# Layer 1's normalised batches: 32x32 block turns on VectorE and copies within SBUF in place of TensorE transposes

## The chip, the core and the metric

The kernel runs on one core of a Trainium2 chip. A core has five engines with instruction streams of their own: TensorE (PE, matrix products, with a separate record PEld for its weight loads), VectorE (DVE), ScalarE (ACT), GpSimd (POOL) and SyncE (SP, which here issues nearly all DMAs). They meet only through semaphores. Data lies in SBUF (128 partitions), matrix products land in PSUM (banks of 128 x 512 f32), and DMAs move data between device memory and SBUF or within SBUF. The metric is the time of one execution on the device in microseconds, median of the runs.

## What is computed

Two transformer layers with adaptive layer norm, on x of 4 batches x 512 tokens x 512 features, all in f32. The change touches layer 1 only:

```python
h = _layernorm(x) * (1 + ca) + sa            # "h" of the attention
x = x + ga * _L1_attn_ref(h, w_q, w_k, w_v, w_o)   # 32 heads of 128, 8 key/value heads, causal, softmax
h = _layernorm(x) * (1 + cb) + sb            # "h" of the FFN
x = x + gb * _L1_ffn_ref(h, gate, up, down)  # silu(h gate^T) * (h up^T), then down^T; width 1792, int weights
```

`sa, ca, ga, sb, cb, gb` are rows of 512 per batch, from a small product with the condition vector. The norm runs over the features of a token. A token sits in a partition when x is normalised, but the matrix products want the features in the partitions, so each normalised batch (512 x 512) has to be turned: 16 blocks of 128 x 128.

## The kernel before

Layer 0 comes first (to about 184 us of the span) and is not touched. Layer 1's attention follows (184 to about 1720 us), then the FFN (to the end). Inside each the order of every engine's instructions is written out by hand (`tc.manual_schedule`): an instruction stands in its engine's queue where the Python code emits it.

**Attention.** The 32 pairs of batch and key/value head are blocks n = 0 to 31 (`NBLK`), b = n // 8, g = n % 8. A block has four query heads; two windows per block handle two heads each: window 2n ("even") and window 2n+1 ("odd"). `window` walks through 9 slots. In slot i it emits the score product of one token tile (`score`: PE product, DVE mask and maximum, ACT exponential), the division of the tile before (`divide`), the 32x32 block turn of the tile two before (`flip`, DVE); in slots 8 and 9 the two products with the values of the previous pair (`value`, tile `av`). Into the slots it spreads a list `fill` of further PE pieces, as evenly as its length allows, and a list `side` of work for other engines. Pieces of the even window are the query projection of block n+1 and a part of a key or value projection; pieces of the odd window are the seven products of the output projection of block n-1 (`o_pieces`; each product is one of the seven of a Strassen scheme, tile `quarter`) and up to three key or value pieces (`now`). A PE piece writes one of three PSUM banks (`bank`, pool `ps_sc`), which DVE or ACT then reads. After a window's slots, `carry` issues 16 DMAs on SP (L918) which move the turned probabilities of a pair within SBUF, 32 partitions x 4 runs of 1 KB each.

Every batch after the first has its layer norm made while the batch before is still in the attention. At g = 4 the batch is read back from device memory (`get`, L990, into tile `xn`). At g = 5 its moments are taken in the even window and ACT normalises it in place (`norm_pieces`, L1004); in the odd window `turn_pieces` puts four pieces among the PE fill, each of four TensorE transposes (L1035, tile `lnT`, one PSUM bank) and an ACT instruction (L1038) that scales, shifts and writes a quarter of `hT`. The fill of every odd window has four places for such pieces; in the blocks without them the places hold empty functions. The tiles `hT` come from a pool of four.

**FFN.** `ffn_exact` goes through the batches; for each, 14 hidden blocks n of 128 (`hidden`). An iteration emits the `gate` and `up` products of block n (8 + 8 products of 512 columns: four chunks of features, each in a high and a low part; L1349), then the `down` products of block n-1 (8, L1368). The chain of block n on the other engines is: ACT sigmoid (L1355), DVE two products (L1356, L1357), ACT rounding to the high part (L122), DVE the low part (L123). PSUM holds four accumulators of 512, one bank for turns (`ps_tr2`) and three banks for gate and up (`ps_hu`). The matrix products of batch b+1 need its normalised, turned, split batch `h2`; `prepare(b + 1)` returns a list of pieces, of which iterations n = 2 on emit one each, behind the products: n = 2 to 5 moments of a token tile, n = 6 the reciprocal deviation (one power on POOL, L68, between two small DVE instructions), n = 7 and 8 the normalisation on ACT (L1306, two tiles each, into the free space of `acc`), n = 9 to 12 one chunk each: four TensorE transposes (L1314), DVE scale and shift (L1318), ACT high part, DVE low part. For batch 0 the same iterations also carry the last batch's attention output (`leave_attention`, POOL additions L972 to L978 and L969, DVE L965) and weight loads with their conversion on POOL (L1338).

Of the kernel before, what the change touches and what calls it, by code (L numbers as in the profile page):

```python
# [8 lines left out]
F32 = mybir.dt.float32  # L9
# [8 lines left out]
P = 128  # L18
# [15 lines left out]
def adaln_two_layers(ctx: ExitStack, tc: tile.TileContext, a, out: bass.AP):  # L34
# [69 lines left out]
    def modulated_T(xn, b, m, shift, scale, hT, on_act, trp):  # L104

        def put(c, pt, sc_, sh_):
            if on_act[c] == "a":
                nc.scalar.activation(hT[:, c, :], pt, AF.Identity, bias=sh_, scale=sc_)
            else:
                nc.vector.tensor_scalar(hT[:, c, :], pt, sc_, sh_, ALU.mult, ALU.add)  # L110

        transposed(xn, b, m, shift, scale, put, trp)
        return hT

    def layernorm_T(b, m, shift, scale, pool, xnp, trp):
        xn = normalized(b, lambda: xnp.tile([P, NT, E], F32, tag="xn", name="xn"))
        hT = pool.tile([P, KC, S], F32, tag="hT", name="hT")
        return modulated_T(xn, b, m, shift, scale, hT, "vava", trp)

    def halves(hi, lo, t):  # L120

# [613 lines left out]
    def bank(shape, name):  # L735
        return ps_sc.tile(shape, F32, tag="sc", name=name)
# [255 lines left out]
    def one_x():  # L992
        return lnp.tile([P, NT, E], F32, tag="xn", name="xn")

    def norm_pieces(xb):
# [7 lines left out]
        def xn(t):  # L1003
            nc.scalar.activation(  # L1004
                xb[:, t, :], xb[:, t, :], AF.Identity,
                bias=out_["nmr"][:, t : t + 1], scale=out_["rstd"][:, t : t + 1],
            )
# [16 lines left out]
        return out_, side + after  # L1024

    def turn_pieces(b, got):

        m = modT[1]

        def piece(c):  # L1030
            if c == 0:
                h1[b] = hp.tile([P, KC, S], F32, tag="hT", name="hT")
            pt = bank([P, S], "lnT")
            for t in range(NT):
                nc.tensor.transpose(  # L1035
                    pt[:, t * P : (t + 1) * P], got["xn"][:, t, c * P : (c + 1) * P], ident
                )
            nc.scalar.activation(  # L1038
                h1[b][:, c, :], pt, AF.Identity,
                bias=m[:, 0, c, b : b + 1], scale=m[:, 1, c, b : b + 1],  # L1040
            )
            if c == KC - 1:
                sums_h(b, (nc.gpsimd, nc.gpsimd))

        return [lambda c=c: piece(c) for c in range(KC)]

    def small_loads():
        nc.sync.dma_start(gus[:, 0], a["L1_ffn_gate_scaleT"])
# [126 lines left out]
    load("v", 1)  # L1175
    pending = []
    begun = []

    for n in range(NBLK):
        b, g = divmod(n, HKV)  # L1180
# [12 lines left out]
        if g == 1 and b > 0:  # L1193
            sums, ends = leave_attention(b - 1, nc.gpsimd, gap, "ga", xb)
            side[0] = sums + 3 * [lambda: None] + ends
            side[1] = put(b - 1, xb)
        if g == HKV - 4:
            xb = one_x()
            side[1] = get(after, xb)
        if g == HKV - 3 and after or n == NBLK - 2:  # L1200
            got, side[0] = norm_pieces(xb)
            if after:
                turns_ = turn_pieces(after, got)
        if 0 < n <= len(pieces):
            found = scan(n - 1)
            side[1] += [lambda j=j: look(n - 1, j, found[j]) for j in range(2)]
# [7 lines left out]
        if n == 0:  # L1214
            window(0, q[:6])
        elif ahead:
            late = [lambda: load("q", n + 2)] if n + 2 < NBLK else []
            if n == 1:
                window(2, q, side[0], late)
            else:  # L1220
                window(2 * n, begun[:2] + q[:2] + begun[2:] + q[2:], side[0], late)
                begun = []
                if 2 * (m + 1) < NBLK:
# [24 lines left out]
        if 0 < n < NBLK - 2:  # L1248
            sums_in("q", n + 2)
        if n == 0:  # L1250
            sums_in("v", 1)
            begun = v_pieces(1)
            window(1, q[6:] + k_pieces(1) + begun[:3], (), [lambda: load("q", 2)])
            begun = begun[3:]
            sums_in("q", 2)
            load("k", 2)
            pending.append(("k", 2))
        else:
            if n > 1 and n + 2 < NBLK:
# [21 lines left out]
    def ffn_exact():  # L1281
        with (
# [11 lines left out]
            def prepare(b):  # L1294


                (st, mv), d, m = moments(), {}, modT[1]
                xn = osum.rearrange("p a b c -> p (a b c)")[:, : NT * E]
                xn = xn.rearrange("p (t e) -> p t e", e=E)

                def dev():
                    d["dev"] = deviation(mv)

                def norm(t):
                    rstd, nmr = d["dev"]
                    nc.scalar.activation(  # L1306
                        xn[:, t, :], x[b][:, t, :], AF.Identity,
                        bias=nmr[:, t : t + 1], scale=rstd[:, t : t + 1],
                    )

                def chunk(c):
                    pt, t = ps_tr2.tile([P, S], F32, tag="tr", name="lnT"), temp()
                    for i in range(NT):
                        nc.tensor.transpose(  # L1314
                            pt[:, i * P : (i + 1) * P], xn[:, i, c * P : (c + 1) * P], ident
                        )
                    sc_, sh_ = m[:, 3, c, b : b + 1], m[:, 2, c, b : b + 1]
                    nc.vector.tensor_scalar(t, pt, sc_, sh_, ALU.mult, ALU.add)  # L1318
# [180 lines left out]
```

## Time and profile before

| | us |
|---|---|
| median of 3 runs (lowest, highest) | 2040.57 (2040.56, 2052.83) |
| the profiled execution: its time / its span | 2043.52 / 2041.6 |
| PE busy / DVE / ACT / POOL | 2006.0 / 1363.2 / 878.8 / 759.5 |
| attention, 184 to 1680: length / PE busy | 1496.00 / 1493.06 |
| FFN, batch 1 (1800.88 to 1878.90): length / PE busy | 78.02 / 78.02 |
| mean granted TensorE clock, of full speed | 0.991 |

The span runs from the first to the last instruction of the profiled execution. A line of the page's list of groups gives the source line, the engine, the operation, output and input tiles with shapes, the count, the busy time and the mean duration, and then how long the engine was idle just before these instructions and who ended that. Timelines give start and duration in us. A merged timeline row "x4" is four instructions; the start of the next row says when the engine went on.

### The profile page before, as it was taken

How to read it: one execution, taken by the hardware profiler on the slowest of the kernel's cores; microseconds unless marked ns; L12 is line 12 of the kernel's file. 1: busy time of each engine (PE TensorE's matmuls, PEld its weight loads, DVE VectorE, ACT ScalarE, POOL GpSimd, SP SyncE). 2: the span in 40 equal slices, each digit the busy share in tenths (PEclk: the TensorE clock that was granted, in tenths of full speed). 3: DMA queues.
4: the chain of work that ended last, by engine and by line, in shares of the span. 5: the costliest groups of instructions: out<-in, count | busy, mean ns of one | idle time of the engine just before them, and what ended most of it. 6: DMA issues, size and time to landing. Idle time of an engine off the chain costs nothing.

```text
span 2041.6 us, 27493 instructions
## 1 busy us (share of the span) xinstructions
PE 2006.0 (98%) x9219; PEld 1571.0 (77%) x9219; DVE 1363.2 (67%) x3317; ACT 878.8 (43%) x2001; POOL 759.5 (37%) x659
## 2 busy tenths in 40 slices
PE   6999999999999999999999999999999999999998
PEld 4555777878788777778787778788777777888887
DVE  6957776676667766766676676667666674755554
ACT  4521554444444444544444444444444454323322
POOL 2316243334346343354463334346343333800000
PEclk8999999999999999999999999999999999999999
DMA  9322566666666756566766665667656656500000
GB/s 316 105 68 99 134 173 162 145 165 148 168 159 179 185 148 165 145 167 159 180 181 155 145 165 141 155 149 175 169 136 155 145 127 213 187 21 6 16 22 22
DMA packets 243640, 288.59 MB, mean 141 GB/s; under 512 B 23250, under 2 KB 184018, under 8 KB 243492
## 3 DMA queue, kind: packets, MB, share of 16 engines
q1 hardware_dynamic: 242964, 285.71, 53.5%
q8 instruction: 76, 1.25, 0.3%
q10 hardware_dynamic: 528, 1.05, 0.1%
q14 instruction: 72, 0.59, 0.1%
HBM read 142.99 MB, written 11.57 MB: 76 GB/s over the span
## 4 chain that ended last, share of the span: by engine, by line
PE 89%; DVE 1%; ACT 1%; SPq 0%; DMA 0%; issue 0%; ACTq 0%
PE quarter L746 47%; PE av L928 14%; PE sc L878 13%; PE p_gate L1349 5%; PE p_up L1349 5%; PE acc L1368 5%; PE lnT L1035 0%; PE lnT L1314 0%; SPq L918 0%; DMA x<-p 0%; DVE nmx L881 0%; ACT x L883 0%; DVE x L1377 0%; ACT tm L1089 0%; DVE tm L1376 0%
## 5 line engine op out<-in xcount | busy, mean ns | idle before, releaser
L878 PE MATMUL sc<-kT,qT 128*128 128x512 f32 (+3 forms) x1024 | 355.4, 433 | 0.8 <-DVE qT L778 0.8
L928 PE MATMUL av<-x,v 128*128 128x512 f32 x1008 | 293.7, 435 | 2.0 <-DMA x<-p 2.0
L928 PEld LDWEIGHTS av<-x,v 128*128 128x128 f32 x1008 | 189.4, 191 | 107.6 <-issue 63.3
L881 DVE TENSOR_REDUCE nmx<-sc 128x1 f32<-128x512 f32 (+3 forms) x512 | 251.3, 491 | 17.7
L893 ACT ACTIVATE x<-x,rden 128x512 f32<-128x512 f32 (+3 forms) x256 | 143.7, 561 | 237.5 <-DVE rden L892 237.5
L778 DVE TENSOR_TENSOR qT<-qT,quarter 128x512 f32<-128x512 f32 x224 | 150.4, 683 | 137.9 <-PE quarter L746 133.1
L893 ACT ACTIVATE p<-p,rden 128x512 f32<-128x512 f32 (+3 forms) x256 | 143.7, 562 | 223.3 <-DVE rden L892 221.8
L879 DVE TENSOR_TENSOR sc<-sc,mask 128x128 f32<-128x128 f32 x512 | 144.9, 283 | 135.0 <-PE sc L878 134.2
L842 DVE TENSOR_TENSOR acc<-acc,quarter 128x512 f32<-128x512 f32 x196 | 134.4, 686 | 132.5 <-PE quarter L746 132.4
L230 POOL TENSOR_TENSOR sq<-wq 128x512 f32<-128x512 f32 x32 | 41.1, 1284 | 477.1 <-DMA wq<-in_L_attn_w_q_dram 458.6
L878 PEld LDWEIGHTS sc<-kT,qT 128*128 128x128 f32 x1024 | 182.7, 191 | 25.5 <-DVE qT L778 1.2
L746 PEld LDWEIGHTS quarter<-wo,oT 128*128 128x128 f32 x744 | 140.9, 190 | 43.9 <-issue 20.1
L883 ACT ACTIVATE p<-sc,nmx 128x512 f32<-128x512 f32 (+3 forms) x256 | 134.9, 527 | 87.0 <-DVE nmx L881 78.6
L746 PE MATMUL quarter<-wo,oT 128*128 128x256 f32 x744 | 171.1, 379 | 0.2 <-ACT oT L933 0.2
L883 ACT ACTIVATE x<-sc,nmx 128x512 f32<-128x512 f32 (+3 forms) x256 | 134.8, 526 | 69.9 <-DVE nmx L881 65.3
L933 ACT COPY oT<-av 128x512 f32<-128x512 f32 x128 | 74.2, 579 | 163.9 <-PE av L928 162.0
L896 DVE STREAM_TRANSPOSE p<-p 128x512 f32<-128x512 f32 (+3 forms) x256 | 129.3, 505 | 1.8
L896 DVE STREAM_TRANSPOSE x<-x 128x512 f32<-128x512 f32 x248 | 124.8, 503 | 1.4 <-ACT x L893 0.9
L746 PEld LDWEIGHTS quarter<-hT,wq 128*128 128x128 f32 x512 | 97.3, 190 | 32.4 <-issue 14.6
L746 PE MATMUL quarter<-hsum,wq 128*128 128x256 f32 x512 | 121.0, 379 | 0.0
L746 PE MATMUL quarter<-hsum,sq 128*128 128x256 f32 x512 | 121.0, 379 | 0.0
L746 PE MATMUL quarter<-hT,wq 128*128 128x256 f32 x512 | 121.0, 379 | 0.0
(256 smaller groups left out, 3733.0 us busy)
## 6 DMA issues: line engine op xcount, KB each, us to landing
x<-p SPq DMA_DIRECT2D x512, 128.0 KB, 3.8
x<-x SPq DMA_DIRECT2D x496, 128.0 KB, 3.7
wq<-in_L_attn_w_q_dram SPq DMA_DIRECT2D x32, 1024.0 KB, 5.8
wo<-in_L_attn_w_o_dram SPq DMA_DIRECT2D x31, 1024.0 KB, 5.6
wm<-in_L_wmod_dram SPq DMA_DIRECT2D x12, 1024.0 KB, 9.5
wk<-in_L_attn_w_k_dram SPq DMA_DIRECT2D x16, 512.0 KB, 4.2
wv<-in_L_attn_w_v_dram SPq DMA_DIRECT2D x16, 512.0 KB, 4.2
xn<-x_d SPq DMA_DIRECT2D x28, 256.0 KB, 5.9
```

Source lines behind the costliest of these rows:

```text
L746: nc.tensor.matmul(ps[:, m, :], l[:, k, m * P : (m + 1) * P], r[:, k, :], start=(k == 0), stop=(k == 1),)
L778: nc.vector.tensor_tensor(c[out], c[v], ps, ADD if sign > 0 else SUB)
L842: nc.vector.tensor_tensor(osum[:, i - 1], osum[:, i - 1], ps, ADD)
L878: nc.tensor.matmul(ps[:, :w], q[:, i * P : w], kT[n][:, :w], start=True, stop=True)
L879: nc.vector.tensor_tensor(ps[:, i * P : w], ps[:, i * P : w], mask, ADD)
L881: nc.vector.tensor_reduce(nmx, ps[:, :w], AX.X, ALU.max, negate=True)
L883: nc.scalar.activation(blocks(s, i), ps[:, :w].rearrange("p (j q) -> p j q", q=BK), AF.Exp, bias=nmx, accum_out=den,)
L893: nc.scalar.mul(p, p, rden)
L896: nc.vector.transpose(blocks(s, i), blocks(s, i))
L928: nc.tensor.matmul(av.rearrange("p (a n) -> p a n", a=NG)[:, :, BK * k :], vs[n][:, k, :], pT[:, k, :, P * (s % 2) + BK * k : P * (s % 2 + ...
L1349: nc.tensor.matmul(ps[kind], w[kind][:, k, c * P : (c + 1) * P], h2[b % 2][i][:, k, :], start=(k == 0 and i == 0), stop=(k == KC - 1 and i ...
L1368: nc.tensor.matmul(acc[t], act[i][:, t * P : (t + 1) * P], w[:, c, :], start=(n == 0 and i == 0), stop=(n == NI - 1 and i == 1),)
```

## The change

In the attention a batch is read back two blocks earlier (g = 2) and normalised at g = 3. ACT writes the normalised tile t into `z`, an `hT` tile with the layout [partition, 4 column groups j of 32, token tile, chunk, 32]. In the odd window of that block DVE turns it in 32x32 blocks, in place, 512 columns per instruction (4 in all). Then SP moves blocks of 32 partitions x 512 within SBUF from `z` to `y` (16 DMAs): 8 behind the carry of this window, 8 behind that of the next even window. At g = 5 ACT reads `y` in four instructions and writes `hT`, in slots 0 to 3 of the odd window. The empty functions leave the fill of all odd windows.

In the FFN the same is done in halves of two chunks, because `y` has the size of half a batch. The moments and the deviation take iterations 2 to 5, normalisation (each tile in two instructions of 256 columns) 6 and 7; behind the second also the 4 block turns of the first half and its 16 DMAs. Iteration 8: the turns of the second half; 9: chunk 0; 10: chunk 1 and the 16 DMAs of the second half into the same `y`; 11: nothing; 12: chunk 2; 13 (the last): chunk 3. The pool for turns goes, and gate and up have four banks.

The last batch of layer 1's attention that is normalised for the FFN (`split_pieces`) and all of layer 0 keep TensorE's transposes.

```diff
+    TURN = [P, P // 32, NT, KC, 32]
+    def place_of(z, t):
+        return z[:, :, t], lambda ap: ap.rearrange("p (c j q) -> p j c q", j=P // 32, q=32)
+    def turn_blocks(z, j):
+        zj = z[:, j].rearrange("p t c q -> p (t c) q")
+        nc.vector.transpose(zj, zj)
+    def move_blocks(z, y, j):
+        for i in range(P // 32):
+            nc.sync.dma_start(y[32 * j : 32 * (j + 1), i], z[32 * i : 32 * (i + 1), j])
+    def chunk_of(y, c):
+        return y[:, :, :, c, :]
...
     def turn_pieces(b, got):
...
-            pt = bank([P, S], "lnT")
-            for t in range(NT):
-                nc.tensor.transpose(
-                    pt[:, t * P : (t + 1) * P], got["xn"][:, t, c * P : (c + 1) * P], ident
-                )
             nc.scalar.activation(
-                h1[b][:, c, :], pt, AF.Identity,
+                in_order(h1[b][:, c, :]), chunk_of(got["y"], c), AF.Identity,
...
-        return [lambda c=c: piece(c) for c in range(KC)]
+        return [p for c in range(KC) for p in (lambda: None, lambda c=c: piece(c))]
...
-        if g == HKV - 4:
+        if g == (HKV - 6 if after else HKV - 4):
...
-        if g == HKV - 3 and after or n == NBLK - 2:
-            got, side[0] = norm_pieces(xb)
+        if g == HKV - 5 and after or n == NBLK - 2:
+            got, side[0] = norm_pieces(xb, after > 0)
             if after:
-                turns_ = turn_pieces(after, got)
+                turns_ = [lambda j=j: turn_blocks(got["z"], j) for j in range(P // 32)]
+        if g == HKV - 3 and after:
+            turns_ = turn_pieces(after, got)
...
+                run(*moves)
+                moves = []
...
-            more = turns_ + 4 * [lambda: None]
-            window(2 * n + 1, o[:3] + now + more[:1] + o[3:4] + more[1:2] + o[4:5] + more[2:3] + o[5:6] + more[3:4] + o[6:], side[1], late)
+            window(2 * n + 1, o[:3] + now + o[3:], turns_ + side[1], late)
+            if g == HKV - 5 and after:
+                moves = move_pieces(got)
+                run(moves.pop(0), moves.pop(0))
...
-            tc.tile_pool(name="ps_tr2", bufs=1, space=PSUM) as ps_tr2,
-            tc.tile_pool(name="ps_hu", bufs=3, space=PSUM) as ps_hu,
+            tc.tile_pool(name="ps_hu", bufs=4, space=PSUM) as ps_hu,
...
                 def chunk(c):
-                    pt, t = ps_tr2.tile([P, S], F32, tag="tr", name="lnT"), temp()
-                    for i in range(NT):
-                        nc.tensor.transpose(
-                            pt[:, i * P : (i + 1) * P], xn[:, i, c * P : (c + 1) * P], ident
-                        )
+                    t = temp()
                     sc_, sh_ = m[:, 3, c, b : b + 1], m[:, 2, c, b : b + 1]
-                    nc.vector.tensor_scalar(t, pt, sc_, sh_, ALU.mult, ALU.add)
+                    nc.vector.tensor_scalar(
+                        in_order(t), chunk_of(y, c % 2), sc_, sh_, ALU.mult, ALU.add
+                    )
                     halves(h2[b % 2][0][:, c, :], h2[b % 2][1][:, c, :], t)
...
-                    [lambda t=t: statistics(b, t, st, mv) for t in range(NT)] + [dev]
-                    + [lambda t=t: (norm(t), norm(t + 1)) for t in (0, 2)]
-                    + [lambda c=c: chunk(c) for c in range(KC)]
+                    [lambda t=t: stats(t) for t in range(3)] + [lambda: (stats(3), dev())]
+                    + [lambda: (norm(0), norm(1)), lambda: (norm(2), norm(3), turned_(0), move(0))]
+                    + [lambda: turned_(1), lambda: chunk(0), lambda: (chunk(1), move(1))]
+                    + [lambda: None, lambda: chunk(2), lambda: chunk(3)]
```

More of the change, by code (lines that the diff above doesn't have):

```diff
@@ L118, in layernorm_T, with in_order @@
         return modulated_T(xn, b, m, shift, scale, hT, "vava", trp)
+    TURN = [P, P // 32, NT, KC, 32]
[9 more added lines that the diff above has]
+        return y[:, :, :, c, :]
+    def in_order(ap):
+        return ap.rearrange("p (t i q) -> p i t q", t=NT, q=32)
     def halves(hi, lo, t):
@@ L993, in one_x, with norm_pieces @@
         return lnp.tile([P, NT, E], F32, tag="xn", name="xn")
-    def norm_pieces(xb):
+    def norm_pieces(xb, blocks_):
         (st, mv), out_ = moments(), {"xn": xb}
@@ L1003, in xn @@
         def xn(t):
+            dst, src = xb[:, t, :], xb[:, t, :]
+            if blocks_:
+                if t == 0:
+                    out_["z"] = hp.tile(TURN, F32, tag="hT", name="xblocks")
+                dst, read = place_of(out_["z"], t)
+                src = read(src)
             nc.scalar.activation(
-                xb[:, t, :], xb[:, t, :], AF.Identity,
+                dst, src, AF.Identity,
                 bias=out_["nmr"][:, t : t + 1], scale=out_["rstd"][:, t : t + 1],
@@ L1024, in norm_pieces, with move_pieces, piece @@
         return out_, side + after
+    def move_pieces(got):
+        def piece(j):
+            if j == 0:
+                got["y"] = hp.tile(TURN, F32, tag="hT", name="xturned")
+            move_blocks(got["z"], got["y"], j)
+        return [lambda j=j: piece(j) for j in range(P // 32)]
     def turn_pieces(b, got):
@@ L1042, in piece @@
             if c == KC - 1:
+                got.clear()
                 sums_h(b, (nc.gpsimd, nc.gpsimd))
-        return [lambda c=c: piece(c) for c in range(KC)]
+        return [p for c in range(KC) for p in (lambda: None, lambda c=c: piece(c))]
     def small_loads():
@@ L1222, in adaln_two_layers @@
                 begun = []
+                run(*moves)
+                moves = []
                 if 2 * (m + 1) < NBLK:
@@ L1297, in prepare @@
                 (st, mv), d, m = moments(), {}, modT[1]
-                xn = osum.rearrange("p a b c -> p (a b c)")[:, : NT * E]
-                xn = xn.rearrange("p (t e) -> p t e", e=E)
+                room = osum.rearrange("p a b c -> p (a b c)")
+                z = room[:, : NT * E].rearrange(
+                    "p (h j t c q) -> p h j t c q", h=2, j=P // 32, t=NT, q=32
+                )
+                y = room[:, NT * E : NT * E + NT * E // 2].rearrange(
+                    "p (i t c q) -> p i t c q", i=P // 32, t=NT, q=32
+                )
                 def dev():
@@ L1305, in norm @@
                     rstd, nmr = d["dev"]
-                    nc.scalar.activation(
-                        xn[:, t, :], x[b][:, t, :], AF.Identity,
-                        bias=nmr[:, t : t + 1], scale=rstd[:, t : t + 1],
-                    )
-                def chunk(c):
-                    pt, t = ps_tr2.tile([P, S], F32, tag="tr", name="lnT"), temp()
-                    for i in range(NT):
-                        nc.tensor.transpose(
-                            pt[:, i * P : (i + 1) * P], xn[:, i, c * P : (c + 1) * P], ident
-                        )
-                    sc_, sh_ = m[:, 3, c, b : b + 1], m[:, 2, c, b : b + 1]
-                    nc.vector.tensor_scalar(t, pt, sc_, sh_, ALU.mult, ALU.add)
+                    for h in range(2):
+                        dst, read = place_of(z[:, h], t)
+                        nc.scalar.activation(
+                            dst, read(x[b][:, t, h * E // 2 : (h + 1) * E // 2]), AF.Identity,
+                            bias=nmr[:, t : t + 1], scale=rstd[:, t : t + 1],
+                        )
@@ new lines, in stats, with turned_, move, chunk @@
+                def stats(t):
+                    statistics(b, t, st, mv)
+                def turned_(h):
+                    for j in range(P // 32):
+                        turn_blocks(z[:, h], j)
+                def move(h):
+                    for j in range(P // 32):
+                        move_blocks(z[:, h], y, j)
+                def chunk(c):
+                    t = temp()
+                    sc_, sh_ = m[:, 3, c, b : b + 1], m[:, 2, c, b : b + 1]
+                    nc.vector.tensor_scalar(
+                        in_order(t), chunk_of(y, c % 2), sc_, sh_, ALU.mult, ALU.add
+                    )
```

## The prediction

> **What bounds the kernel now.** I read the list of engines first, then the chain that ended last.
>
> ```profile
> PE 2006.0 (98%) x9219; PEld 1571.0 (77%) x9219; DVE 1363.2 (67%) x3317; ACT 878.8 (43%) x2001; POOL 759.5 (37%) x659
> ...
> PE 89%; DVE 1%; ACT 1%; SPq 0%; DMA 0%; issue 0%; ACTq 0%
> ```
>
> PE is busy for 2006.0 of 2041.6 us and makes nearly the whole chain: an instruction taken from PE is time saved, unless PE then waits. The busy time by window shows how much the others have left (columns: window, length, then busy us and count of PE, PEld, DVE, ACT, POOL; clock; DMA share):
>
> ```profile
> 454.86:480.01 25.15, 25.15 (x130) 20.43 (x129) 18.68 (x51) 14.44 (x34) 5.09 (x4) 1.00 0.59 147
> 504.31:527.61 23.30, 23.30 (x101) 18.36 (x101) 15.58 (x40) 9.47 (x24) 6.60 (x7) 1.00 0.65 159
> 1800.88:1878.90 78.02, 78.02 (x353) 64.63 (x352) 42.57 (x65) 23.69 (x36) 6.11 (x5) 1.00 0.04 14
> ```
>
> The first is an odd window of the attention with turns, the second one without, the third a batch of the FFN. PE has no idle time in any of them, at full clock.
>
> **What goes.** PE's timeline prices a group of four transposes by the start of the row behind it: in the attention, then in the FFN, then an FFN product without transposes ahead.
>
> ```profile
> 470.76 0.60 PE L1035 MATMUL lnT<-ident,xn 128*128 128x128 f32 x4
> 471.19 1.89 PE L746 MATMUL quarter<-so,soT 128*128 128x256 f32 x8
> ...
> 1783.16 0.60 PE L1314 MATMUL lnT<-ident,acc 128*128 128x128 f32 x4
> 1783.51 2.08 PE L1349 MATMUL p_gate<-h,gate 128*128 128x512 f32 x8
> 1785.44 1.98 PE L1349 MATMUL p_up<-h,up 128*128 128x512 f32 x8
> ...
> 1800.88 1.98 PE L1349 MATMUL p_gate<-first,gate 128*128 128x512 f32 x8
> 1802.69 1.98 PE L1349 MATMUL p_up<-first,up 128*128 128x512 f32 x8
> ```
>
> Attention: 0.43 us a group, four groups in each of three batches: 5.2 us. FFN: 0.35 us, and the gate product behind it takes 1.93 instead of 1.81, so 0.47 us; 12 groups: 5.6 us. Together **-10.8 us**. An iteration of the FFN without transposes is 24 products of 0.227 us (1.81 / 8): 5.44 us.
>
> The Trainium skill, "VectorE: DVE Perf Modes", "Rules for kernel authors", speaks against this change: turn 128x128 on TensorE where PSUM may be the destination; "The three transpose paths" gives 390 ns for one in bf16. By that figure the 96 would be 37 us; the rows above, four f32 turns in 0.43, decide here.
>
> **What comes in the attention.** Per batch: four block turns on DVE; the row for 128x512 (L896) has 0.706 us, so 2.8 us in an odd window where DVE is busy 15.6 of 23.3. It stays under PE's time; within slots 2 to 4 DVE gets about 2.6 us of work per slot against PE's 1.1 to 1.75 and falls behind by at most some 4 us, and four score banks and three others hold about two slots each. Cost 0; without that cover at most the 2.8 us, three times. ACT's four reads move from PSUM to SBUF and come earlier. SP issues 16 more DMAs in two lots of 8, behind a carry. What waits behind them on SP is scan and weight loads; the queue's own waits show their slack:
>
> ```profile
> SPq L208 <- PE quarter L746: 560.5, 59, 11.8
> ```
>
> SP waits 9.5 us on average for PE before such a load, the lots take 4 to 5 us: hidden. The read-back and the moments move two blocks earlier into windows built alike. Without empty functions the fill's 9 slots go from 2,2,2,1,1,0,1,0,1 real pieces to 2,1,1,1,1,1,1,1,1; PE has no idle there to win. Net of the attention **-5.2**.
>
> **What comes in the FFN.** Here two things are on the path. First, the last chunk is now made in iteration 13, the one before the batch whose products need it; before it was 12. The rows of the DVE chain, in an iteration whose p_gate starts at 1783.51 and then, without transposes, at 1800.88:
>
> ```profile
> 1788.89 0.69 DVE L123 TENSOR_TENSOR act_lo<-tm,act_hi 128x512 fp32r<-128x512 f32 x1 [0.69 <-ACT act_hi L122]
> 1789.70 0.81 DVE L1318 TENSOR_SCALAR tm<-lnT,modT 128x512 f32<-128x512 f32 x1
> 1791.20 0.69 DVE L123 TENSOR_TENSOR first<-tm,first 128x512 fp32r<-128x512 f32 x1 [0.69 <-ACT first L122]
> ...
> 1806.14 0.69 DVE L123 TENSOR_TENSOR act_lo<-tm,act_hi 128x512 fp32r<-128x512 f32 x1 [0.69 <-ACT act_hi L122]
> ```
>
> Count from the start of iteration 13. The low part of its own block ends at 1806.83 - 1800.88 = 5.95; chunk 3 starts 0.12 later (1789.58 to 1789.70), at 6.07; ACT's high part starts 0.85 behind it and takes 0.62: 7.54; the low part ends 2.19 behind it: 8.26. PE comes to the next batch at 5.44 and to chunk 3's high product, the seventh, at 5.44 + 6 x 0.227 = 6.80: it waits 0.75, then at the low one another 0.5. **1.3 us per batch** with 0.05 for a semaphore. (L1318 read PSUM; from SBUF it may be shorter, then 0.9.)
>
> Second, the moves. DMA issue is not in this place of the trace. Two rows of SP bound its pitch, seven of the carry (32 partitions x 4 runs, within SBUF) and four of the read-back (128 partitions, one run each):
>
> ```profile
> 419.46 4.50 SPq L918 DMA_DIRECT2D x<-x  x7
> 424.00 0.59 SPq L208 DMA_DIRECT2D wv<-in_L_attn_w_v_dram  x1
> 424.69 1.92 SPq L990 DMA_DIRECT2D xn<-x_d  x4
> ```
>
> 0.64 and 0.48 us. The moves are within SBUF from 32 partitions like the first, with one run per partition like the second. I take 0.48, since the number of runs is where the first two differ most plainly, and keep 0.33 (one output store alone, L1378) to 0.64. Landing: 2.3, the carry's shortest; the stores have 2.1.
>
> Count from the start of iteration 7, batches 1 and 2. ACT's high part of block 7 ends at 5.2; the halves of the normalisation lie between 0.38 (half of 0.76, two tiles in 1.52 on L1306) and 0.51 us (128x256 on L893), say 0.45, and the first half of the columns is complete after the third: 6.6. Four turns of 0.44: the first done at 7.1, when the DMAs start. The 16th goes at 7.1 + 15 x 0.48 = 14.3 and lands at 16.6. Chunk 0's place on DVE is two iterations on: 10.88 + 6.07 = 16.95. On time. Chunk 1 has read `y` at 16.32 + 6.07 + 0.81 = 23.2; the second moves land at 23.25 + 7.2 + 2.3 = 32.75; chunk 2's place is 27.2 + 6.07 = 33.27. On time by half a microsecond. Both hold up to a pitch of 0.50. At 0.64 chunk 0 is 2.1 late, chunk 1 with it, chunk 2 lands 4.2 late, and behind chunk 2 on DVE and ACT wait block 13 and then chunk 3: PE waits 1.3 + 4.1 = 5.4 us per batch.
>
> The Trainium skill, "DMA: Bandwidth & Descriptors", "Anatomy of one DMA", gives some 50 ns for the sequencer's dispatch and 2.0 us fixed. By its 50 ns the 16 moves would all be out in 0.8 us, both chunks would be in time in every batch, and the sum would be -5.7; the shortest of the two rows above has ten times that, so the rows decide.
>
> **Batch 0** is worse, since POOL still adds the attention's output. The deviation moves from iteration 6 to 5, and its power on POOL comes right behind the last addition, which ends at 1761.76; with DVE's small instruction ahead (1.0 us long there) and 1.02 for itself it ends at about 1763.3. DVE waits for it, and behind it the product of gate 6, which ran at 1761.13: 2.3 us later. Its high part moves from 1763.35 to 1765.6; PE wants it at 1764.10: 1.5 us. Before, the same wait one iteration on cost PE some 0.3. So +1.2. DVE is also slowed by POOL in these iterations (the low part took 1.33 and 1.20 instead of 0.69), so I put chunk 2 at 1.9 late: 3.2 instead of 1.3. Bounds of both: 0 to 7.
>
> FFN: -5.6 + 2 x 1.3 + 3.2 + 1.2 = **+1.4**. The turns there (24 of 0.44: 10.6 us) and the doubled ACT instructions lie beside PE; DVE's load is 43 of 78.
>
> **Sum:** -5.2 + 1.4 = -3.8 us. The profiled execution, 2043.52 (span 2041.6 and 1.9 around it), becomes 2039.7. The median of the runs is 2.9 lower, 2040.57, so **2036.8**, say 2037.
>
> **Rivals.**
>
> *The moves are paced like the carry* (0.64). For: same direction, same 32 partitions, and a carry's first DMA, with nothing close ahead, already takes 0.59. Against: one run instead of four. 5.4 in batches 1 and 2, 7.3 in batch 0 and 1.2: 19.3 us lost, -10.8 + 19.3 = +8.5: **2049**, slower than before. It decides from a pitch of 0.50 on; break-even is at about 0.55.
>
> *No wait at the batch's end.* If chunk 3 is served earlier than I have it (a shorter L1318, DVE out of step by less), only fractions stay: **2030**. Against: the program order on DVE, where block 13 stands ahead.
>
> *The odd windows turn on DVE.* Their new spacing puts pieces where scores are short; should DVE's lag outgrow the PSUM banks, PE waits in all 30. At 0.4 us each, +12: 2048 if the rest holds. Against: 7.7 us of idle DVE in each.
>
> *The gain isn't there in the attention:* PE, relieved, shows the 5.2 us as idle behind DVE in the three windows: -3.8 + 5.2 = +1.4, 2042. The 96 transposes themselves are gone from PE's program in any case.
>
> **How the numbers follow.** Forecast 0.5 (2033 to 2041), carry's pace 0.27, no wait 0.13, odd windows 0.06, gain lost 0.04. The range takes in both ends of the pitch, and so both larger rivals: 2029 to 2049. All terms are below 1% (20 us), about what a measurement of this kernel can tell from no change: within 1% 0.93. Slower by over 1% 0.05, for a wait in every window or a pitch over the carry's; faster 0.02.
>
> **What would show it.** PE's count of matrix instructions falls by 96; the odd window of g = 5 shrinks from 25.15 to 23.4 us. Moves: pitch on SP near 0.48. PE's waits list p_gate behind ACT `first` and DVE `first` at the start of batches 1 to 3, 1.3 us in two of them. An FFN batch takes 76.2 + 1.3 = 77.5 instead of 78.0. Wrong would be the sum if SP's pitch is over 0.5 (chunk 2 on DVE then waits for DMA), or if PE shows idle in odd windows of the attention.

## The result, and the profile after

The changed kernel is slower: **2064.42 us** median of 15 runs (2054.68 to 2069.56) beside 2042.00 for the kernel before on the same chip (15 runs, 2038.98 to 2052.83); ratio **1.0078**, 95% interval 1.0061 to 1.0094, so about 16 us. The runs of either kernel fall into two groups some 10 us apart (before 2038.98 to 2042.22 and 2049.59 to 2052.83, after 2054.68 to 2059.29 and 2064.42 to 2069.56), and the two medians lie in different ones; within either group the change costs some 15 us, and both profiled executions are near the lower one. The loss lies within 1%, as was given the highest chance, but on the other side of the sign and above the range (2037; 2029 to 2049). The profiled execution took 2055.97 us, 12.45 more than that of before.

First the page of the changed kernel: engines, and the chain that ended last.

```profile
PE 2001.7 (97%) x9123; PEld 1564.0 (76%) x9123; DVE 1364.2 (66%) x3353; ACT 880.9 (43%) x2013; POOL 760.1 (37%) x659
...
PE 82%; DVE 3%; SPq 2%; ACT 1%; DMA 1%; issue 0%; POOL 0%; DVEq 0%; ACTq 0%
PE quarter L770 46%; PE av L952 13%; PE sc L902 13%; PE p_up L1409 3%; PE p_gate L1409 3%; PE acc L1428 3%; SPq L135 2%; DMA wi<-in_L_ffn_down_wqT_dram 1%; DVE tm L1417 0%; DVE act_lo L147 0%; DMA acc<-acc 0%; ACT act_hi L146 0%; DVE tm L1416 0%; DVE acc L131 0%; DVE tm L1375 0%
```

The 96 matrix instructions are gone from PE (9219 to 9123), but its busy time fell by only 4.3 us. The chain has new members: SP's queue at L135 (the moves) with 2%, DMAs with 1%, DVE with 3%. The busy time by window (columns as in the prediction): the odd window of g = 5 in the first of the three batches, then batches 1 and 2 of the FFN:

```profile
450.69:474.09 23.40, 23.40 (x113) 18.77 (x113) 15.84 (x41) 12.72 (x30) 10.45 (x9) 1.00 0.62 158
1795.27:1883.09 87.82, 80.15 (x338) 64.86 (x337) 44.49 (x74) 25.17 (x42) 6.08 (x5) 0.94 0.09 27
1883.09:1964.83 81.74, 78.32 (x337) 64.17 (x336) 44.62 (x74) 25.03 (x41) 6.09 (x5) 0.98 0.09 26
```

The attention did what was forecast: 25.15 became 23.40 us, PE without idle time at full clock. The FFN did not: its batches take 87.8 and 81.7 us instead of 78.0, PE is idle for 7.7 and 3.4 us of them, and the granted clock is 0.94 and 0.98, where it was 1.00. PE's busy time in them is longer as well (80.2 instead of 78.0, with 15 instructions fewer): its products ran at a slower pace for a while. What PE waited for from the end of the attention on (total us, times, longest):

```profile
PE p_gate L1409 <- ACT first L146: 10.2, 3, 4.5
PE p_gate L1409 <- ACT h L146: 3.2, 1, 3.2
PE acc L1428 <- ACT act_hi L146: 2.9, 2, 2.3
...
PE p_gate L1409 <- DVE acc L866: 0.9, 1, 0.9
```

The first two rows are the first gate products of batches 1 to 3, waiting for late chunks of their batch's input. ACT only passes the wait on; what it waited for is DVE's L1375 (the chunk's scale and shift), and that waited for the moves (source view of L135, then waits of ACT and DVE):

```profile
L135 SPq DMA_DIRECT2D acc<-acc x96: 507/588/1546, 1765.3 to 1961.0; - x96
L135 SPq DMA_DIRECT2D xturned<-xblocks x48: 564/589/890, 395.6 to 1185.9; - x48
...
ACT first L146 <- DVE tm L1375: 28.8, 8, 9.9
DVE tm L1375 <- DMA acc<-acc: 22.9, 6, 8.5
```

A move occupies SP for 0.59 us, and from one start to the next it is 0.633 us (median of neighbours), in the attention and in the FFN alike. The prediction had taken 0.48.

The same traces cut into stretches, from the starts of PE's products (columns 2 and 3 in us):

| stretch | before | after | difference |
|---|---|---|---|
| start to the second block's first `av` product | 268.75 | 264.57 | -4.2 |
| attention, from there to the last block's | 1427.77 | 1422.37 | -5.4 |
| to the first gate product of the FFN | 27.32 | 29.00 | +1.7 |
| FFN, first to last group of gate products | 301.99 | 321.11 | +19.1 |
| to the end | 15.72 | 17.13 | +1.4 |

The first row is no work of the change: in the kernels below it lies between 264.6 and 277.4 us whatever their edits. The last row isn't either (15.5 to 17.2). Without these two the change cost 15.4 us, which is what the ratio says.

### The profile page after: what moved, and what is told of

Same layout as the page of the kernel before. It is cut to its first block, busy times and chain, and to the rows that moved or that the text cites. A ratio compares the mean times of both kernels' runs of the same rounds, so it can differ in the third digit from the quotient of the medians.

```text
span 2054.2 us, 27525 instructions
## 1 busy us (share of the span) xinstructions
PE 2001.7 (97%) x9123; PEld 1564.0 (76%) x9123; DVE 1364.2 (66%) x3353; ACT 880.9 (43%) x2013; POOL 760.1 (37%) x659
## 4 chain that ended last, share of the span: by engine, by line
PE 82%; DVE 3%; SPq 2%; ACT 1%; DMA 1%; issue 0%; POOL 0%; DVEq 0%; ACTq 0%
PE quarter L770 46%; PE av L952 13%; PE sc L902 13%; PE p_up L1409 3%; PE p_gate L1409 3%; PE acc L1428 3%; SPq L135 2%; DMA wi<-in_L_ffn_down_wqT_dram 1%; DVE tm L1417 0%; DVE act_lo L147 0%; DMA acc<-acc 0%; ACT act_hi L146 0%; DVE tm L1416 0%; DVE acc L131 0%; DVE tm L1375 0%
## 5 line engine op out<-in xcount | busy, mean ns | idle before, releaser
L902 PE MATMUL sc<-kT,qT 128*128 128x512 f32 (+3 forms) x1024 | 360.0, 433 | 0.8 <-DVE qT L802 0.8
L866 DVE TENSOR_TENSOR acc<-acc,quarter 128x512 f32<-128x512 f32 x196 | 134.2, 685 | 135.6 <-PE quarter L770 135.4
```

Source lines behind the costliest of these rows:

```text
L866: nc.vector.tensor_tensor(osum[:, i - 1], osum[:, i - 1], ps, ADD)
L902: nc.tensor.matmul(ps[:, :w], q[:, i * P : w], kT[n][:, :w], start=True, stop=True)
```

## The experiments

The table gives, for all kernels but two measuring ones further down, the ratio to the kernel before and, from the trace, the length of the FFN iterations in which most waits fell (5.44 us without a wait) and the length of the FFN as in the table above. Outside these columns, "FFN only" lost 2.75 us in iteration 11 of batch 0, and "batch 0's order" 1.3, 2.6 and 4.3 us in iterations 9, 11 and 13.

| kernel | ratio (95%) | batch 0, iteration 7 | first iteration of batch 1, 2, 3 | FFN |
|---|---|---|---|---|
| before | 1 | 5.58 | 5.44, 5.44, 5.44 | 301.99 |
| after | 1.0078 (1.0061 to 1.0094) | 9.62 | 17.09, 11.03, 8.76 | 321.11 |
| attention only | 0.9978 (0.9958 to 0.9999) | 5.44 | 5.44, 5.44, 5.44 | 301.99 |
| FFN only | 1.0106 (1.0081 to 1.0132) | 7.08 | 17.11, 8.54, 8.62 | 318.04 |
| moves left out | 0.9982 (0.9960 to 1.0003) | 9.30 | 6.39, 6.41, 6.41 | 303.17 |
| moves earlier | 0.9950 (0.9929 to 0.9972) | 5.44 | 5.44, 5.44, 5.44 | 298.06 |
| two queues | 1.0025 (1.0008 to 1.0041) | 9.43 | 11.30, 6.41, 6.42 | 308.16 |
| batch 0's order | 1.0051 (1.0035 to 1.0068) | 5.56 | 10.31, 10.73, 8.87 | 317.97 |

The theory after the result: the FFN loses because the moves take 0.63 us each on SP and come too late, because chunk 3 is made an iteration later than before, because of a wait behind POOL in batch 0, and because PE runs at half pace for a while after a longer wait. The rivals: DVE and ACT, with more to do, are themselves too slow or in the wrong order; or the two halves of the change disturb one another.

### Attention only, FFN only

The first is the changed kernel with before's `ffn_exact`:

```diff
-            tc.tile_pool(name="ps_hu", bufs=4, space=PSUM) as ps_hu,
+            tc.tile_pool(name="ps_tr2", bufs=1, space=PSUM) as ps_tr2,
+            tc.tile_pool(name="ps_hu", bufs=3, space=PSUM) as ps_hu,
...
-                    + [lambda: None, lambda: chunk(2), lambda: chunk(3)]
+                    + [lambda c=c: chunk(c) for c in range(KC)]
```

The second is the reverse: before's attention, the changed `ffn_exact`, and the helpers that it calls:

```diff
...
+    def turn_blocks(z, j):
+    def move_blocks(z, y, j):
+    def chunk_of(y, c):
+    def in_order(ap):
```

> Only the attention's half of the change, the FFN as before. Theory (the loss lies in the FFN alone): three odd windows shorter by 1.75 us each, so 5.3 us less than before, ratio 0.9974, no wait of TensorE for DVE that before does not have. Rival (the relieved TensorE shows the gain as idle time elsewhere in the attention, or the spaced-out fill costs it): no difference from before, ratio 1.000.

> Only the FFN's half of the change, the attention as before. Theory: the whole loss and 5.3 us more than the changed kernel has, so some 22 us over before, ratio 1.0105; TensorE's waits of the FFN as in the changed kernel (some 17 us). Rival (the halves disturb one another, through the place of the norm or of the weights' loads): clearly less than that, below 15 us.

Measured 0.9978 and 1.0106. In the trace of the first, the products with the values come 1.75 us earlier behind each of the three windows and keep their distance to those of before in between; the FFN is as long as before to the hundredth. In the second, PE's waits from the FFN's first product on sum to 17.6 us, and from the second block to the end its trace is 18.7 us longer than that of before. So the halves add up by the ratios (-0.0022 + 0.0106 = 0.0084, beside 0.0078), and the loss is the FFN's alone. The two FFN stretches, 318.04 and 321.11, still differ by 3.1 us: in the second kernel batch 0 loses 1.6 and 2.75 us in iterations 7 and 11 instead of 4.2 in iteration 7, and batch 2's wait of 2.5 us is not followed by half pace.

### The moves left out

```diff
                 def move(h):
-                    for j in range(P // 32):
-                        move_blocks(z[:, h], y, j)
+                    pass
...
-                        in_order(t), chunk_of(y, c % 2), sc_, sh_, ALU.mult, ALU.add
+                        in_order(t), chunk_of(z[:, c // 2], c % 2), sc_, sh_, ALU.mult, ALU.add
```

> The changed kernel without the FFN's 96 DMAs within SBUF: the chunks read the blocks where DVE turned them, so that the exchange of blocks between partitions is left out and the result is another. Everything else (turns, doubled ACT instructions, places in the iterations) stays. Theory (late moves are the larger part): waits at the start of batches 1 to 3 fall from 11.6, 5.6 and 3.3 us to about 1.3 each; the wait in batch 0 behind the deviation stays, with about 4.5 us; with 5.6 + 5.3 saved and 3 lost at the FFN's two ends the time comes out at before's, within 3 us. Rival (the load of DVE and ACT or the order on them makes the waits): the time stays at the changed kernel's, some 16 us over before.

Measured 0.9982: some 20 us below the changed kernel, with all of DVE's turns and ACT's doubled instructions still there. PE's timeline at the start of batch 1:

```profile
1803.94 1.52 PE L1408 MATMUL p_gate<-first,gate 128*128 128x512 f32 x6
1805.62 0.49 PE L1408 MATMUL p_gate<-first,gate 128*128 128x512 f32 x1 [0.16 <-ACT first L146]
1806.35 0.50 PE L1408 MATMUL p_gate<-first,gate 128*128 128x512 f32 x1 [0.23 <-DVE first L147]
1806.68 2.00 PE L1408 MATMUL p_up<-first,up 128*128 128x512 f32 x8
```

Six products run, the seventh (chunk 3's high part) and the eighth (its low part) wait: the place that the prediction named. The iteration is 0.95 to 0.97 longer than 5.44, against 1.3 forecast. Batch 0's iteration 7 stays long (9.30), so that loss has nothing to do with the moves. The time came out a little below the forecast (before's, within 3 us): the ratio gives 3.7 us less.

### The moves earlier

```diff
-                    [lambda t=t: stats(t) for t in range(3)] + [lambda: (stats(3), dev())]
+                    [lambda: (stats(0), stats(1)), lambda: (stats(2), stats(3), dev())]
                     + [lambda: (norm(0), norm(1)), lambda: (norm(2), norm(3), turned_(0), move(0))]
-                    + [lambda: turned_(1), lambda: chunk(0), lambda: (chunk(1), move(1))]
-                    + [lambda: None, lambda: chunk(2), lambda: chunk(3)]
+                    + [lambda: turned_(1), lambda: None, lambda: chunk(0), lambda: (chunk(1), move(1))]
+                    + [lambda: None, lambda: None, lambda: (chunk(2), chunk(3))]
...
+                if b == 1:
+                    return (
+                        [lambda t=t: stats(t) for t in range(NT)] + [dev]
+                        + [lambda t=t: (plain(t), plain(t + 1)) for t in (0, 2)]
+                        + [lambda c=c: by_pe(c) for c in range(KC)]
+                    )
```

`plain` and `by_pe` are the normalisation and the chunk of the kernel before, with its two PSUM pools. So batch 1 is prepared as before the change, by TensorE's transposes, and only batches 2 and 3 test the earlier moves.

> The changed kernel with the FFN's moves begun two iterations earlier for batches 2 and 3 (statistics paired, chunk 0 in iteration 8, chunks 2 and 3 both in iteration 12), and batch 1's four chunks turned by TensorE as before, with before's PSUM banks. Same moves, same pace, same turns on DVE. Theory (the moves are only too late, and chunk 3 one iteration too late): no wait of p_gate for ACT or DVE at a batch's start; 5.3 saved in the attention and 8 x 0.47 = 3.8 in the FFN, 9.0 us below before, ratio 0.9956. Rival (the load of DVE and ACT makes the waits): p_gate still waits at the start of batches 2 and 3 and the time is over before's less 5 us.

Measured **0.9950**: faster than the kernel before. From the second block to the end its trace is 9.2 us shorter than before's, 3.9 of them in the FFN. Batches 1 and 2 of its FFN, by window:

```profile
1801.75:1877.91 76.16, 76.16 (x338) 63.08 (x336) 43.35 (x72) 23.97 (x39) 6.09 (x5) 1.00 0.10 28
1877.91:1954.07 76.16, 76.16 (x338) 63.08 (x336) 43.94 (x73) 24.58 (x40) 6.10 (x5) 1.00 0.10 28
```

No idle time, full clock, 1.87 us less than before in each, 0.47 per group of transposes as the prediction had it. The moves are the same, at the same pace; those of the first half begin two iterations earlier, those of the second half one place earlier in the list, and chunk 3 is made in iteration 12 again. What each of these three is worth alone was not tried. The rival falls: DVE has 43 to 44 us of work in each batch and gets it done beside PE.

### What makes the pitch

Six lots of eight DMAs in the kernel before, to a part of `acc` that nothing reads, each of 192 elements a partition.

```diff
+                    dst = room[:, NT * E + W * i : NT * E + W * (i + 1)]
+                    if kind == "sbuf128":
+                        nc.sync.dma_start(dst, x[b][:, i % NT, :W])
...
+                    if kind == "sbuf32runs":
+                        nc.sync.dma_start(
+                            dst[:32].rearrange("p (t q) -> p t q", t=NT),
+                            x[b][q, :, 48 * i : 48 * (i + 1)],
+                        )
+                    if kind == "dram32":
+                        nc.sync.dma_start(dst[:32], x_d[b, q, i % NT, :W])
```

L1388, L1390 and L1392 are the lots within SBUF from 128, 64 and 32 partitions, L1394 that of four runs, L1399 and L1401 those from device memory to 32 and 128 partitions.

> The kernel before, with six lots of 8 additional DMAs of 192 elements a partition on SP's queue in the FFN, to an unused room: within SBUF from 128, 64 and 32 partitions, within SBUF from 32 partitions in four runs each, and from DRAM to 32 and to 128 partitions. Theory (both ends in SBUF make the pitch): 0.63 us for all four lots within SBUF, 0.48 or less for both lots from DRAM. Rival 1 (32 partitions make it): 0.63 for the lots of 32 partitions, also from DRAM, 0.48 for that of 128 within SBUF. Rival 2, the prediction's own reading (the number of runs makes it): 0.63 only for the lot with four runs.

SP's timeline (a row "x8" gives the eight together):

```profile
1811.84 5.07 SPq L1388 DMA_DIRECT2D acc<-x  x8
1816.95 5.03 SPq L1392 DMA_DIRECT2D acc<-x  x8
...
1889.91 3.67 SPq L1399 DMA_DIRECT2D acc<-x_d  x8
1893.63 3.75 SPq L1401 DMA_DIRECT2D acc<-x_d  x8
...
1967.96 5.47 SPq L1390 DMA_DIRECT2D acc<-x  x8
1973.47 5.22 SPq L1394 DMA_DIRECT2D acc<-x  x8
```

The pitch, median of the seven neighbours, is 0.644, 0.640 and 0.633 us from 128, 64 and 32 partitions within SBUF and 0.644 with four runs; 0.464 and 0.474 from device memory to 32 and 128 partitions. The partitions and the runs move it by 0.011 at most; where the source lies moves it by 0.17. (The destination was SBUF in all six lots. The kernel's time was 1.0016 of before's, 0.9997 to 1.0035.) The prediction's reading of its two rows is refuted.

### Two queues

```diff
+                        for i in range(P // 32):
+                            eng = nc.gpsimd if i % 2 else nc.sync
+                            eng.dma_start(
+                                y[32 * j : 32 * (j + 1), i], z[32 * i : 32 * (i + 1), h, j]
+                            )
```

> The changed kernel with every second DMA of the FFN's moves issued by GpSimd's queue, so that 16 of them need half the time to issue. Bytes, places and everything else stay. Theory (SP's pitch makes the moves late): the first product group of batches 2 and 3 takes about 6.4 us as without moves, instead of 11.0 and 8.8; batch 1's falls too, but is held by the loads of weights on SP; 7 to 13 us below the changed kernel, so 3 to 9 over before. Rival (the transport or the landing makes them late): no shorter than the changed kernel.

Measured 1.0025, some 11 us below the changed kernel. Batches 2 and 3 begin exactly as with no moves at all (6.41 and 6.42), so there nothing but SP's pitch made them late. GpSimd's own pitch for the same moves is 0.49 us. Batch 1 keeps 11.30, and here the second queue brings a delay of its own: SP begins its half of the second moves at 1791.07, but GpSimd's half stands behind GpSimd's conversion of the weights, and DVE waits 4.07 us for the moves:

```profile
1798.73 1.04 POOL L1402 CAST down<-wi 128x1024 fp32r<-128x1024 int32 x1
1799.72 3.95 POOL L1372 DMA_DIRECT2D acc<-acc  x8
```

The next experiment is about batch 1 with SP alone; both edits together were not tried.

### Batch 0's order

```diff
+                if b == 1:
+                    first += [lambda: stats(3), dev]
+                    first += [lambda: ([norm(t) for t in range(NT)], turned_(0), move(0))]
...
-                    if b == 0 and n % NC_ == 0 and n // NC_ + 2 <= NB:
+                    if b == 0 and n % NC_ == 0 and n // NC_ + 2 < NB:
...
+                    if b == 0 and n // NC_ + 2 == NB and n % NC_ == 0:
+                        load(0)
```

> The changed kernel with two edits for what batch 0 prepares: the deviation back in iteration 6 (all four normalisations in 7, the moves where they were), and the load of weight block 0 behind the second moves in iteration 10 and no longer ahead of them. Theory: the product group of iteration 7 falls from 9.6 to about 6 us, since DVE no longer waits for the power behind POOL's additions, and batch 1's first from 17.1 to about 11 us, since SP no longer waits for a buffer of the weights ahead of the moves and they no longer share the transport with the weights: some 9 us below the changed kernel, so 7 over before, ratio 1.003. Rival (batch 1's start is late by the pitch alone, as in batches 2 and 3): the first group stays near 17 us.

Measured 1.0051. The first edit did its part: iteration 7 fell from 9.62 to 5.56. The second, which puts the load behind the pieces of iteration 10, took 6.8 us from batch 1's first iteration (17.09 to 10.31) and gave back more than half of them just ahead of it. SP's queue in the changed kernel, from its timeline:

```profile
1765.32 10.08 SPq L135 DMA_DIRECT2D acc<-acc  x16
...
1783.48 0.37 SPq L1394 DMA_DIRECT2D wi<-in_L_ffn_down_wqT_dram  x1
1783.95 14.34 SPq L135 DMA_DIRECT2D acc<-acc  x16
```

and what came of it on DVE:

```profile
1799.55 0.55 DVE L1375 TENSOR_SCALAR tm<-acc,modT 128x512 f32<-128x512 f32 x1 [8.53 <-DMA acc<-acc]
```

The second 16 moves, which start when chunk 1 has been read (1782.47 + 1.26), take 14.3 us instead of 10.1 and land up to 8.5 us after their issue instead of 1.8 to 1.9: they share the transport with the load of weight block 0 just ahead. The load's last part lands at 1792.69, and moves issued at 1784.51 to 1785.83 land right behind it, at 1793.06 to 1793.39. SP's DMAs also take turns at eight semaphores in this kernel, and a move is issued only when the DMA eight places ahead has landed: the seventh goes at 1791.40, where the load's second part landed at 1791.39, the eighth at 1792.70. With the load behind them the 16 take 10.5 us and land within 3.3, so the load ahead was the cause. But then the load itself is late, and PE waits for it ahead of batch 1's first product (the wait counts in iteration 13 of batch 0, 9.75 us):

```profile
1799.29 2.93 PE L1415 MATMUL p_gate<-first,gate 128*128 128x512 f32 x6 [4.14 <-POOL gate L1404]
1803.15 1.52 PE L1415 MATMUL p_gate<-first,gate 128*128 128x512 f32 x2 [0.93 <-ACT first L146]
```

Beside that, iterations 9 and 11 of batch 0 lost 1.3 and 2.6 us; whether the four normalisations in one iteration cause it was not tried apart. Of the expected 9 us some 5 came by the ratio and 3 by the trace: in neither of the two orders tried do both the load and the 16 moves fit between chunk 1 and the next batch.

### The wait by itself

The kernel before, with nothing of the change, but with DVE kept busy ahead of one product in seven iterations.

```diff
+            extra = {
+                (1, 3): 9, (1, 6): 10, (2, 3): 11, (2, 6): 11,
+                (3, 3): 12, (3, 6): 13, (3, 9): 15,
+            }
+            spare = moments()[0]
...
+                    for _ in range(extra.get((b, n), 0)):
+                        nc.vector.bn_stats(spare[:, 0, :], x[b][:, 0, :])
                     act = hidden(b, n)
```

> The kernel before, with nothing of the change, but with 9, 10, 11, 11, 12, 13 and 15 additional statistics instructions on VectorE (results unused, about 0.70 us each) ahead of one product of the FFN in seven iterations, so that TensorE has to wait for some 0.9, 1.6, 2.3, 2.3, 2.2, 2.9 and 4.3 us, 16.5 us in all. Theory (a wait of TensorE over about 2.4 us is followed by products at 0.43 instead of 0.23 us for some 4 us, so that it costs about 2 us more than itself): half pace behind the longest two and some of the 2.3, none behind 0.9 and 1.6; total 16.5 + 4 to 8, ratio 1.010 to 1.012. Rival (the half pace seen in the changed kernel comes of its DMAs within SBUF or of DVE's turns): products at 0.23 us behind every wait, total 16.5, ratio 1.008.

Measured 1.0172 (1.0150 to 1.0194). The FFN is 27.2 us longer, above both figures given: PE is idle for 18.1 us ahead of the seven products and not 16.5, and some 9 us come on top. The rest of the ratio lies mostly at the start (277.4 us here). The 3 us behind each of four waits, by window; by the distance of two products' starts, less the 0.227 us of a product, the waits are 1.9, 2.7, 2.6 and 4.8 us:

```profile
1854.40:1857.40 3.00, 3.00 (x13) 2.23 (x14) 1.46 (x3) 1.21 (x2) 0.78 (x1) 1.00 0.00 0
1940.20:1943.20 3.00, 3.00 (x9) 2.34 (x8) 1.18 (x4) 1.21 (x2) 1.02 (x1) 0.50 0.00 0
2005.90:2008.90 3.00, 3.00 (x13) 2.25 (x14) 2.21 (x4) 1.21 (x2) 0.00 (x0) 1.00 0.00 0
2048.60:2051.60 3.00, 3.00 (x7) 2.41 (x8) 2.08 (x3) 1.21 (x2) 0.00 (x0) 0.50 0.00 0
```

Half clock and 7 to 9 products instead of 13 behind the second and the fourth, full clock behind the first and the third. There is no DMA and no turn of the change in this kernel, so the half pace comes of the wait. The lengthening of the iteration less the wait is 0.3 us without half clock (three waits) and 1.6 to 2.1 with it (four).

## Why the prediction was wrong

**The step that failed: "I take 0.48, since the number of runs is where the first two differ most plainly."** The two rows differ in their source too, one from SBUF and one from device memory, and that is what counts: the moves went at 0.633 us, and lots from device memory at 0.464 to 0.474. (No lot measured here shows the 50 ns a DMA that the prediction quoted and set aside.) The rival with the carry's pace was the right one, and its condition too (it decides from 0.50 on). At 0.64 it had chunk 0 late by 2.1 and chunk 2 by 4.2 us (some 4.0 by its own rows); DVE waited 2.07 and 3.65 for them in batch 1 and 2.64 and 2.94 in batch 2.

**But the rival too was sized too small:** +8.5 us, where the change cost about 15.4. Its terms, against the traces:

| term | forecast or rival | measured |
|---|---|---|
| attention, three windows | -5.2 | -5.26 |
| transposes of the FFN | -5.6 | -5.6 (1.87 a batch with the moves earlier) |
| chunk 3 an iteration later | 1.3 a batch | 0.95 to 0.97 |
| first iterations of batches 2 and 3 | rival 5.4 each | 5.6 and 3.3 |
| first iteration of batch 1 | rival 7.3 | 11.65 |
| batch 0's wait behind POOL | 1.2 | 4.2, and 0.45 in the next iteration |
| entry to the FFN | none | 1.7 |

- *Chunk 3's place* was right; L1375 takes 0.55 us from SBUF where it took 0.81 from PSUM, and with that shorter instruction the prediction itself had 0.9.
- *Batch 0's moves:* the contention with the weights' load was in no step. The prediction asked, for the attention, what waits behind the moves on SP, and not what is in flight when they go.
- *Batch 0's wait:* the mechanism was right (with the deviation back in iteration 6 it is gone). Forecast was a wait of 1.5 against 0.3 before; it was 2.5, and behind it the products ran at half pace.
- *The half pace* was in no term, the rivals' included. By the distances of the products' starts it makes up some 1.6 us in batch 0, 2.2 at the start of batch 1 and 1.6 at that of batch 2; batch 3's start, with a wait of 2.65 us, had none. So that the rival's 5.4 met batch 2's 5.6 is luck: the waits there come to 4.0, and without half pace batch 3 has 3.3. The busy time by window of the changed kernel, at this wait, behind it, and further on:

```profile
1756.00:1759.00 3.00, 0.69 (x3) 0.19 (x1) 1.85 (x3) 1.19 (x3) 1.86 (x2) 1.00 0.01 3
1759.20:1763.50 4.30, 4.29 (x12) 3.39 (x13) 1.69 (x3) 2.63 (x6) 0.00 (x0) 0.60 0.00 0
1763.90:1767.00 3.10, 3.10 (x15) 2.57 (x14) 2.20 (x7) 1.93 (x4) 0.00 (x0) 1.00 0.05 11
```

- *Entry to the FFN:* the first gate product waits 0.9 us for DVE's reading of `quarter` (L866), in all five kernels with four banks for gate and up and in none with before's banks; the stretch takes 29.0 to 29.2 us in those five and 27.3 to 28.5 in the others. So 0.9 of the 1.7 is this wait, and the rest is no more than the others differ among themselves. The prediction priced the change of PSUM pools at nothing and did not say so.

What held: 96 instructions fewer, the odd window at 23.40 us, no cost of the spaced-out fill, DVE's turns beside PE, and the list of signs: a pitch over 0.5 with DVE's chunk waiting for a DMA was named as what would make the sum wrong.

## What to carry to other kernels

When a transfer replaces work of the bounding engine, count the DMAs times their pitch on the queue, take the pitch from a row of the same queue with the same source memory, and place the last landing against the consumer; where it is late by a microsecond or two, begin the chain earlier rather than hope. When the bounding engine is TensorE, reckon with the price of its clock behind a new wait of some 2.4 us or more: here 1.6 to 2.1 us beyond the wait, always from 3.1 us on and half of the time between 2.4 and 2.8. And look at which transfers are in flight at the place where new ones are put, not only at the queue that issues them.

## What the runs showed of the hardware

- **The clock after a wait.** Over all traces of this case, waits of PE in the FFN of 0.76 to 1.93 us were never followed by half clock (products every 0.43 instead of 0.227 us; eight such waits, not counting one that fell into a stretch of half clock; a wait is here the distance of two products' starts less 0.227), those of 3.1 us and more always (ten, two of them close behind another wait); between 2.4 and 2.8 us it was five with and five without, and 2.40 us was enough once where 2.80 was not another time. The Trainium skill, "TensorE: Matmul & The Clock Gate", "Part 1: The HAM clock gate", has a free-running activity window of about 3.4 us, which fits the chance in the middle, and 426.7 ns from start to start for a cold product of 512 columns, which agrees with the measured 0.43. Its section "HAM oscillation — how this bites in real kernels" warns of idle gaps over about 3.4 us; here a wait of 2.40 (2.24 of it idle by the profile) was enough, and the measurement decides.
- **SP's pitch** is 0.63 to 0.64 us for a DMA within SBUF and 0.46 to 0.47 for one from device memory to SBUF, whatever the partitions or runs tried. GpSimd's queue issued the same moves within SBUF at 0.49.
- **The start varies.** Up to layer 1's second block the same instructions took 264.6 to 268.8 us in five profiled executions and 273.5 to 277.4 in five others; in the first 100 us the granted clock lay between 0.76 and 0.95. Kernels a few us apart are compared better by stretches of their traces than by single times.
